# Routed expert results weighted at the copy and added up in DRAM by the scatter; absorbed weights formed in fewer, wider products

## The chip, the cores and the metric

One core of a Trainium2 chip runs the whole program in one launch. The metric is the device time of the launch in microseconds (us). The engines are named as the profile names them: PE (TensorE, matmuls; PEld its weight loads), DVE (VectorE), ACT (ScalarE), POOL (GpSimd) and SP (SyncE, which here only issues transfers); "POOLq", "SPq" and "ACTq" are what their sequencers do besides computing.

## The reference

`x` is [16, 56, 256] in float32, which is 896 tokens of 256 numbers; `ctx_512` is [16, 1500, 64]. Four layers each add a gated attention and a gated feed-forward part, both on a layer norm of `x`:

```python
x = x + tanh(g_xattn[l]) * xattn_l(layernorm(x), ctx_512, ...)
x = x + tanh(g_ffn[l])   * ffn_l(layernorm(x), ...)
```

Attention of layers 1 to 3 is over 1500 rows with 16 heads and heavily factored weights; cut to what matters:

```python
q_hk  = (hidden_q @ Wq.T).reshape(b, s, 16, 128)
q_big = einsum('bshk,hkq->bshq', q_hk, w_kc_q)      # 192 per head; layer 2 rotates it here
q_r   = einsum('bshq,hqr->bhsr', q_big, W_qr)
k_r   = einsum('bld,hdr->bhlr', kv_rope, W_kr)
attn  = softmax(einsum('bhsr,bhlr->bhsl', q_r, k_r))
ctx_c = einsum('bhsl,bld->bhsd', attn, kv_rope)
out   = einsum('bhsd,hkd->bshk', ctx_c, w_kc_kv).reshape(b, s, 2048) @ Wo.T
```

The feed-forward parts are mixtures of experts in layers 0, 2 and 3 (layer 1 has one 8-bit matrix). Layer 0 has 16 experts, the 4 best per token weighted by their softmax, plus two shared experts; layer 3 the same with weights normalised to one, and none shared:

```python
top_w, top_idx = top_k(softmax(logits), 4)
top_w = top_w / sum(top_w)                           # layer 3 only
out = sum over the 4 choices of  top_w * (silu(x @ gate_e) * (x @ up_e)) @ down_e
```

Layer 2 has 8 experts and takes the best one, weighted by a sigmoid.

## The kernel before, in words

The tokens lie in SBUF as `x`, 8 token tiles of 112 tokens. The Python program emits instructions in the order in which it is written; `in_order` and `pin` keep that order, so each engine's queue is what the loops below write, one after the other. Transfers of SP are one queue, those of POOL another.

**Absorbed weights.** `absorbing` (lines 242 to 305) makes, for a pair of heads, one matrix that takes the normalised tokens straight to the query against the rotated context. In layers 1 and 3 four products (float32, two records each in the profile) of `wqr` and `wkr` give `e` [96, 2, 2, 64] (line 280, copied by ACT at 282), four more with `wkc` give `f` (288, copied by DVE at 290), four with `wq` give `M` (297, ACT at 299); two of `wo` and `wkv` give `G` (304). In layer 2, where the rotation stands between, `Mr` is made by eight products (258, 259, ACT copies of 384 columns at 260), and `er` by four of 64 columns (265) with three ACT operations, two of which mask a half by a column of `small`. `queries` (320) calls it for group g+1 between the projections of group g (`project`, line 337); the first two or three groups are made earlier: at the end of layer 0's experts for layer 1, of layer 2's for layer 3, and in the 8-bit layer for layer 2. `load_heads` (224) loads the factors through SP.

**Routing.** `Router.token_tile` (915; layers 2 and 3) and `token_tiles` (1018; layer 0, two tiles at a time) normalise the tokens, rank the experts, count with triangular products at which place of which expert each choice stands, and copy the token's row once per choice into `xr` [112, 4, 257]: 256 numbers and one more, the number of the row (token, choice) in which the result is wanted. Four indirect transfers from POOL scatter these into `rows` in DRAM, sorted by expert (1007, 1100). Before that `clear_rows` (1151) has written zeros over `rows`, 16 transfers of 899.5 KB on SP during layer 0's attention. Behind the scatter the weight of each choice is picked (`weight`), and `finish_weights` (1143) multiplies it by the gate (in layer 3 after dividing by the sum).

**Experts.** `moe` (1159) works on tiles of 128 sorted rows. `table` says which expert a tile belongs to. Layer 0 runs 34 tiles without a condition and layer 3 runs 36; the few tiles beyond stand under a condition on the counted number, which was not met in the profiled execution (34 + 8 + 36 = 78 scatters are seen). Per tile, in a software pipeline of `tiles` (1277): SP loads `wgu`, `wd` and `xrow` three tiles ahead into four buffers each; `turn` transposes the rows (1205, ACT copy 1207) and DVE forms the destination `to` (1209: number plus a mask that pushes rows of no token out of bounds); `hidden` multiplies by gate and up (1217), ACT applies silu (1221), DVE multiplies (1222); `turn_hidden` transposes (1228, 1230); `down` multiplies (1239), ACT copies to `y` (1241, three buffers), and POOL scatters the 128 rows of 1 KB into `results` [896, 4, 256] in DRAM (1242). A bound skips rows out of range, and `declare_no_dep` states that two scatters never write the same row, so that no scatter waits for another.

**What POOL does beside it.** In layer 0 POOL also makes a part of the context's rope table (lines 874, 879, 880), one piece each third tile. In layers 0 and 3, every second one of the last tiles, it makes four diagonal matrices of a token tile's weights (1311), for the tiles in `by_pe`, 6 in layer 0 and 5 in layer 3.

**The end of the experts.** After the condition, PE makes absorbed weights of the next layer (`nxt.absorb`). SP loads `back`, eight transfers of 448 KB (1346), which wait for all scatters. `occupy` (115) issues bfloat16 products of ones that nobody reads. Then each token tile's four results are weighted and summed: tiles in `by_pe` by four products with the diagonals (1359) and a DVE addition (1369), the others by four DVE operations (1372). In layer 3 ACT's queue then sends each tile out (1374); in layers 0 and 2 `nxt.tile` (210) does the next layer norm, whose result PE transposes for the queries.

Of the kernel before, what the change touches and what calls it, by code (L numbers as in the profile page):

```python
# [47 lines left out]
H = 16  # L48
# [3 lines left out]
DQ = 192  # L52
# [6 lines left out]
DX = D + 1  # L59
FAR = 65536.0  # L60

C_U, C_BASE, C_J, C_D4, C_D1, C_ROW, C_C, C_E, C_CAND, C_P, C_M, C_H, C_N = 0, 112, 128, 132, 164, 172, 215, 216, 217, 218, 219, 221, 223
# [12 lines left out]
def flamingo_kernel(ctx: ExitStack, tc: tile.TileContext, d: dict, out: bass.AP):  # L75
# [38 lines left out]

    def occupy(n):

        ps = misc()
        for _ in range(n):
            in_order(nc.tensor.matmul(ps, onesb[:, 0:128], onesb, start=True, stop=True))
    dram = ctx.enter_context(tc.tile_pool(name="dram", bufs=1, space=bass.MemoryType.DRAM))  # L120
    rows = dram.tile([16 * CT, 128, DX], F32, name="rows")
    results = dram.tile([B * S, 4, D], F32, name="results")
# [101 lines left out]
    def load_heads(name, src, g):  # L224
# [3 lines left out]
        room = {"wkc": 512}.get(name, size)  # L228
        w = wpool.tile([128 if name == "wkc" else p, room], F32, tag=name, name=name)[0:p, 0:size]
# [12 lines left out]
    def absorbing(l, g, G, pool, made, pin):  # L242
# [6 lines left out]
        if l == 2:  # L249
# [3 lines left out]
            for k in range(2):  # L253
                ps = misc()
                for j in range(2):
                    lhsT = wq[:, j, k * 128 : (k + 1) * 128]
                    rest = ps[:, 256:384].rearrange("p (b j c) -> p j b c", b=2, j=2)[:, j]
                    pin(nc.tensor.matmul(ps[:, j * 128 : (j + 1) * 128], lhsT, wkc[:, j, 0:128], start=True, stop=True))
                    pin(nc.tensor.matmul(rest, lhsT, wkc[:, j, 128:192].rearrange("p (b c) -> p b c", b=2), start=True, stop=True))
                pin(nc.scalar.copy(M[:, k, :], ps[:, 0:384]))  # L260
                yield
            ps = misc()
            for j in range(2):
                for lhsT, o in ((wqr[:, j, :], 0), (wqr[:, 2, :], 128)):
                    pin(nc.tensor.matmul(ps[:, o + j * DC : o + (j + 1) * DC], lhsT, wkr[:, j, :], start=True, stop=True))
            e = pool.tile([128, 2, 128], F32, name="er", bufs=bufs)
            pin(nc.scalar.copy(e[:, 0, :], ps[:, 0:128]))
            for j in range(2):
                pin(nc.scalar.activation(
                    e[:, 1, j * DC : (j + 1) * DC], ps[:, 128 + j * DC : 128 + (j + 1) * DC], AF.Copy, scale=small[:, C_H + j : C_H + j + 1]  # L270
                ))
            yield
            made[g] = M, e
        else:

            ps = misc()
            for j in range(2):
                for i in range(2):
                    c = (2 * j + i) * DC
                    pin(nc.tensor.matmul(ps[0:96, c : c + DC], wqr[:, j, i * 96 : (i + 1) * 96], wkr[:, j, :], start=True, stop=True))  # L280
            e = pool.tile([96, 2, 2, DC], F32, name="e")
            pin(nc.scalar.copy(e.rearrange("p j i c -> p (j i c)"), ps[0:96, 0 : 4 * DC]))
# [3 lines left out]
            for j in range(2):  # L286
                for i in range(2):
                    pin(nc.tensor.matmul(ps[:, j * DC : (j + 1) * DC], wkc[:, j, i, :], e[:, j, i, :], start=i == 0, stop=i == 1))
# [97 lines left out]
    def attention_mha(router, roping):  # L386
        with ExitStack() as st:
# [51 lines left out]
            clear = clear_rows(ap1)  # L439
# [208 lines left out]
    def attention_mla(l, nxt, router=None, behind_queries=None):  # L648

        with ExitStack() as st:  # L650
# [173 lines left out]
            for k in range(n + 2):  # L824
# [18 lines left out]
                for i in range(6):  # L843
                    if new and i == 2:
                        new.exps1()
                        new.invert()
                    if turn:
                        turn.turned(i)
                if val and val.j == nq - 1:
# [46 lines left out]
    class Router:  # L896
# [18 lines left out]
        def token_tile(self, t):  # L915
# [12 lines left out]
            c = C_D4 + 4 * t if top == 4 else C_D1 + t  # L928
            in_order(nc.gpsimd.tensor_copy(xr[:, :, D : D + 1], small[0:TP, c : c + top].unsqueeze(2)))
# [64 lines left out]
            place = pool.tile([TP, n_e], F32, name="place")  # L994
            in_order(nc.vector.tensor_tensor(place, before, small[0:TP, C_BASE : C_BASE + n_e], ALU.add))
            yield
            is_j = pool.tile([TP, top, n_e], F32, name="is_j")
# [3 lines left out]
            in_order(nc.vector.tensor_tensor(is_j, bcast(rank, 1, top), bcast(small[0:TP, C_J : C_J + top], 2, n_e), ALU.is_equal))  # L1001
# [12 lines left out]
            in_order(nc.vector.tensor_tensor(is_j, is_j, bcast(p, 1, top), ALU.mult))  # L1014
            in_order(nc.vector.tensor_reduce(self.weight[:, t, :], is_j, AX.X, ALU.add))
            yield "end"

        def token_tiles(self, t, n):
# [20 lines left out]
            for u in range(n):  # L1039
# [3 lines left out]
                c = C_D4 + 4 * (t + u)  # L1043
                in_order(nc.gpsimd.tensor_copy(xr[:, u, :, D : D + 1], small[0:TP, c : c + top].unsqueeze(2)))
# [32 lines left out]
            self.total = so_far[n]  # L1077
            yield
# [10 lines left out]
            is_j, prod = tmp("is_j", top, n_e), tmp("prod", top, n_e)  # L1089
            place, slot = tmp("place", n_e), tmp("slot", top)  # L1090
            in_order(nc.vector.tensor_tensor(is_j, bcast(rank, 2, top), bcast(bcast(small[0:TP, C_J : C_J + top], 2, n_e), 1, n), ALU.is_equal))
# [15 lines left out]
            in_order(nc.vector.tensor_tensor(is_j, is_j, bcast(p, 2, top), ALU.mult))  # L1107
            in_order(nc.vector.tensor_reduce(self.weight[:, t : t + n, :], is_j, AX.X, ALU.add))
# [34 lines left out]
        def finish_weights(self):  # L1143
            if self.l == 3:
# [14 lines left out]
    def moe(r, nxt=None, tail=None, rest=None):  # L1159
# [5 lines left out]
        with ExitStack() as st:  # L1165
# [184 lines left out]
            def add_up(t):  # L1350

                if t not in by_pe:
                    return
# [331 lines left out]
```

## Time and profile before

| what | value |
|---|---|
| median of three runs | 2435.41 us (2428.84 to 2443.81) |
| profiled execution | 2433.22 us |
| its span | 2431.4 us, 48119 instructions |
| mean granted TensorE clock | 0.956 of full speed |
| layer 0's expert tiles, first to last scatter | 193.6 to 310.9 us (34) |
| layer 3's expert tiles, first to last scatter | 2293.6 to 2405.5 us (36) |
| diagonals on POOL (line 1311) | 44, 24.1 us |
| sums on PE (line 1359) | 88 records, 21.0 us |
| loads of `back`, layers 0 and 3 | 16 of 448 KB |

The page divides the span into 40 slices of 60.8 us and gives a digit for each engine and slice, the busy share in tenths. A group's row gives the line, engine, operation, the tiles out<-in, the count, busy us, mean ns of one, and how long the engine sat idle before and what ended it. In the chain of waits the columns are start, length and what; in rows of the trace "DMA to landing" counts from the issue of a transfer until its completion is signalled.

### The profile page before, as it was taken

The page shows a single profiled execution, that of the slowest core. Times are in us where ns is not written, and L with a number is a line of the kernel's source. Part 1 is how long each engine was busy: PE and PEld are TensorE (multiplying, and loading weights), DVE is VectorE, ACT ScalarE, POOL GpSimd, SP SyncE. Part 2 cuts the span into 40 slices and gives each one's busy share as a digit, 9 for nine tenths or more (in the row PEclk, how much of TensorE's full clock was granted, in tenths as well). Part 3 has the DMA queues.
Part 4 walks back from the last instruction along what each step waited for, and adds up shares of the span by engine and source line. Part 5 has one row for each costly group of instructions (what it writes and reads, how often), then busy time and mean ns, then how long its engine had stood idle before and what let it go on. Part 6 is the DMA issues. An engine that isn't in the chain of part 4 may idle for free. (4 is left out here: it accounts for less than half of the span.)

```text
span 2431.4 us, 48119 instructions
## 1 busy us (share of the span) xinstructions
PE 2273.1 (93%) x18034; PEld 1648.4 (68%) x18034; DVE 1507.5 (62%) x3384; ACT 1234.8 (51%) x2705; POOL 411.8 (17%) x707
## 2 busy tenths in 40 slices
PE   8678988999999998989999999979899999999687
PEld 5445665777777776447777777755577777777454
DVE  4752335667666667767777777724477777777222
ACT  4312325666666662346666666612566666665231
POOL 4454810000000001430000000001001111111223
PEclk9769988999999998999999999989899999999899
DMA  7736742000000002100000000045200000000497
GB/s 215 220 97 183 222 132 75 22 22 22 21 21 22 22 23 61 35 28 22 22 24 23 24 24 23 11 153 166 61 22 16 27 26 28 28 29 17 151 282 207
DMA packets 114115, 171.93 MB, mean 71 GB/s; under 512 B 20154, under 2 KB 75971, under 8 KB 112852
## 3 DMA queue, kind: packets, MB, share of 16 engines
q1 hardware_dynamic: 104342, 150.30, 20.4%
q0 software_dynamic: 7600, 17.14, 2.2%
q8 instruction: 145, 2.38, 0.4%
q10 hardware_dynamic: 1934, 1.34, 0.2%
q14 instruction: 94, 0.77, 0.1%
HBM read 130.19 MB, written 40.48 MB: 70 GB/s over the span
## 5 line engine op out<-in xcount | busy, mean ns | idle before, releaser
L734 ACT ACTIVATE p<-s_ps,nm 128x500 f32<-128x500 f32 x504 | 335.7, 675 | 396.8 <-DVE nm L725 396.8
L723 DVE TENSOR_REDUCE part<-s_ps 128x1 f32<-128x500 f32 x504 | 340.5, 677 | 262.9 <-PE s_ps L711 262.7
L711 PE MATMUL s_ps<-kvT,qT 64*128 64x500 f32 x2016 | 484.4, 607 | 13.7 <-ACT p L734 6.3
L785 PEld LDWEIGHTS m_ps<-pT,kv 125*64 125x64 f32 x8064 | 436.7, 137 | 76.7 <-issue 69.5
L785 PE MATMUL m_ps<-pT,kv 125*64 125x128 f32 x8064 | 477.3, 275 | 2.2 <-ACT pT L778 1.7
L711 PEld LDWEIGHTS s_ps<-kvT,qT 64*128 64x128 f32 x2016 | 185.5, 189 | 198.4 <-issue 121.1
L773 PE MATMUL m_ps<-ident,p 128*125 128x128 f32 x2016 | 299.4, 283 | 0.3
L728 DVE TENSOR_REDUCE nm<-s_ps 128x1 f32<-128x1500 f32 x168 | 287.1, 1709 | 2.3 <-PE s_ps L711 2.3
L773 PEld LDWEIGHTS m_ps<-ident,p 128*125 128x125 f32 x2016 | 249.4, 188 | 36.5 <-issue 27.0
L743 ACT ACTIVATE p<-s_ps,nm 128x1500 f32<-128x1500 f32 x168 | 254.9, 1517 | 1.3 <-DVE nm L728 0.8
L773 PE MATMUL s_ps<-ident,p 128*125 128x128 f32 x2016 | 251.3, 275 | 0.0
L754 POOL TENSOR_TENSOR den<-den 128x1 f32<-128x1 f32 x168 | 33.4, 199 | 1217.7 <-ACT p L734 1217.4
L773 PEld LDWEIGHTS s_ps<-ident,p 128*125 128x125 f32 x2016 | 237.1, 190 | 0.0
L778 ACT COPY pT<-s_ps 125x512 f32<-125x512 f32 x336 | 181.2, 598 | 90.6 <-PE s_ps L773 76.7
L778 ACT COPY pT<-m_ps 125x512 f32<-125x512 f32 x336 | 185.7, 620 | 0.0
L1217 PE MATMUL gu_ps<-wgu,xT 128*128 128x448 f32 (+2 forms) x344 | 144.0, 546 | 21.2 <-DMA wgu<-in_L_wgu 14.7
L796 DVE TENSOR_TENSOR ctxT<-m_ps,rep 64x128 f32<-64x128 f32 (+1 forms) x384 | 104.4, 272 | 88.4 <-PE m_ps L785 81.6
L1222 DVE TENSOR_TENSOR act<-gu_ps,act 128x224 f32<-128x224 f32 (+2 forms) x78 | 31.2, 400 | 193.3 <-ACT act L1221 193.3
L318 ACT COPY qT<-q_ps 64x224 f32<-64x224 f32 x128 | 71.8, 561 | 109.3 <-PE q_ps L362 71.0
L776 DVE COPY pT<-m_ps 125x512 f32<-125x512 f32 x168 | 116.2, 691 | 10.0 <-PE s_ps L773 0.4
L776 DVE COPY pT<-s_ps 125x512 f32<-125x512 f32 x168 | 114.3, 680 | 0.0
L1217 PEld LDWEIGHTS gu_ps<-wgu,xT 128*128 128x128 f32 x344 | 63.9, 195 | 72.3 <-issue 31.4
(289 smaller groups left out, 2651.2 us busy)
## 6 DMA issues: line engine op xcount, KB each, us to landing
wgu<-in_L_wgu SPq DMA_DIRECT2D x36, 448.0 KB
rows<-zero SPq DMA_DIRECT2D x16, 899.5 KB
kvT<-turned_kv SPq DMA_DIRECT2D x16, 750.0 KB
wgu<-in_L_wgu SPq DMA_DIRECT2D x34, 352.0 KB
rep<-through SPq DMA_DIRECT2D x336, 32.0 KB
xrow<-rows SPq DMA_DIRECT2D x78, 128.5 KB
wgu<-in_L_wgu SPq DMA_DIRECT2D x8, 1024.0 KB
wd<-in_L_wd SPq DMA_DIRECT2D x36, 224.0 KB
```

What stands on the lines that cost most here:

```text
L318: nc.scalar.copy(o, i)
L711: in_order(nc.tensor.matmul(o[:, 0 : 4 * KP], qT[64 * b : 64 * b + 64, t, j * QT : (j + 1) * QT], kvTs[t][64 * b : 64 * b + 64, z * 4 * KP ...
L723: in_order(nc.vector.tensor_reduce(self.part[:, z : z + 1], sp0[z][:, 0 : 4 * KP], AX.X, ALU.max))
L728: in_order(nc.vector.tensor_reduce(self.nm[1], sp1[:, :, 0 : 4 * KP], AX.XY, ALU.max, negate=True))
L734: in_order(nc.scalar.activation(self.p[0][:, 4 * z * KP : 4 * (z + 1) * KP], sp0[z][:, 0 : 4 * KP], AF.Exp, bias=self.nm[0], accum_out=sel ...
L743: in_order(nc.scalar.activation(self.p[1].rearrange("p (z c) -> p z c", z=3), sp1[:, :, 0 : 4 * KP], AF.Exp, bias=self.nm[1], accum_out=se ...
L773: in_order(nc.tensor.transpose(ps[:, c, :], self.p[b][:, k : k + KP], ident))
L776: in_order(nc.vector.tensor_copy(o, ps))
L778: in_order(nc.scalar.copy(o, ps))
L785: in_order(nc.tensor.matmul(self.pv[64 * b : 64 * b + 64, :], kv[:, self.t, c, b, :], self.pT[:, c, b, :], start=c == 0, stop=c == KC - 1))
L796: in_order(nc.vector.tensor_tensor(ctxs[self.t][64 * a : 64 * a + 64, b, lo - 448 * a : hi - 448 * a], self.pv[64 * b : 64 * b + 64, cols] ...
L1217: in_order(nc.tensor.matmul(ps[:, s, 0:n], xT[:, k, :], wgu[:, k, s * n : (s + 1) * n], start=k == 0, stop=k == 1))
```

## The change

In layers 0 and 3 (`SUMMED`) the row that is scattered to the experts carries two numbers beside its values: the token's number and the choice's weight. ACT's copy of `y` multiplies by that weight, taken from the row's last column. The scatter then adds into DRAM, into one of two sums of [1024, 256] that start as zeros, tile i into sum i % 2. Rows of no token go to 128 spare rows behind the 896. The declaration of no dependence is gone for these scatters, since different choices of a token meet in one row: each scatter waits for the landing of the earlier one into the same sum, that is of the tile two before; the program's order of instructions shows this wait in POOL's queue.

At the end of the experts two transfers of 224 KB per pair of token tiles bring the sums back (eight in all), POOL adds the two sums of a pair, and DVE multiplies by the gate (layer 3: gate over the sum of weights) and adds to `x`, one operation per token tile. The diagonals, PE's sums, and layer 3's 30 products of `occupy` are gone. Layer 2 keeps the plain scatter, into [896, 1, 256], and takes the same loop in pairs.

The router picks the weights before it uses the places: in layer 3 two DVE operations and a POOL copy more ahead of the scatter of rows, in layer 0 ahead of the counting products. Four clears of 1.05 MB are added on SP: two before the clears of `rows`, two inside layer 1's attention. `xrow` has seven buffers instead of four.

The absorbed weights: in layers 1 and 3 `wqr` and `wkc` are multiplied first, four products of 128 columns, two heads side by side, and one product with a block-diagonal `wkr` replaces the other four. In layer 2 four products of 192 columns and two of 128 replace eight and four, with five ACT copies per group as before (four of them smaller, one of 256 columns), and no masking.

The diff, cut to its core:

```diff
-DX = D + 1
+DX = D + 2
+SUMMED = (0, 3)
...
-    results = dram.tile([B * S, 4, D], F32, name="results")
+    results = dram.tile([B * S, 1, D], F32, name="results")
+    summed = {l: [dram.tile([B * S + 128, D], F32, name=f"summed{l}{i}") for i in range(2)] for l in SUMMED}
...
             for k in range(2):
-                ps = misc()
+                ps = misc()[:, 0 : 2 * DQ].rearrange("p (j c) -> p j c", j=2)
                 for j in range(2):
-                    lhsT = wq[:, j, k * 128 : (k + 1) * 128]
-                    rest = ps[:, 256:384].rearrange("p (b j c) -> p j b c", b=2, j=2)[:, j]
-                    pin(nc.tensor.matmul(ps[:, j * 128 : (j + 1) * 128], lhsT, wkc[:, j, 0:128], start=True, stop=True))
-                    pin(nc.tensor.matmul(rest, lhsT, wkc[:, j, 128:192].rearrange("p (b c) -> p b c", b=2), start=True, stop=True))
-                pin(nc.scalar.copy(M[:, k, :], ps[:, 0:384]))
+                    pin(nc.tensor.matmul(ps[:, j, :], wq[:, j, k * 128 : (k + 1) * 128], wkc[:, j, :], start=True, stop=True))
+                pin(nc.scalar.copy(M[:, k, 0:256].rearrange("p (j c) -> p j c", j=2), ps[:, :, 0:128]))
+                rest = M[:, k, 256:384].rearrange("p (b j c) -> p j b c", b=2, j=2)
+                pin(nc.scalar.copy(rest, ps[:, :, 128:DQ].rearrange("p j (b c) -> p j b c", b=2)))
...
-            for j in range(2):
-                for i in range(2):
-                    c = (2 * j + i) * DC
-                    pin(nc.tensor.matmul(ps[0:96, c : c + DC], wqr[:, j, i * 96 : (i + 1) * 96], wkr[:, j, :], start=True, stop=True))
-            e = pool.tile([96, 2, 2, DC], F32, name="e")
+            for i in range(2):
+                for j in range(2):
+                    pin(nc.tensor.matmul(
+                        ps[64 * j : 64 * j + 64, 0:128], wqr[:, j, i, :], wkc[:, j, i, :], start=i == 0, stop=i == 1, skip_group_check=True
+                    ))
+            e = pool.tile([128, 128], F32, name="e")
...
-            for j in range(2):
-                for i in range(2):
-                    pin(nc.tensor.matmul(ps[:, j * DC : (j + 1) * DC], wkc[:, j, i, :], e[:, j, i, :], start=i == 0, stop=i == 1))
+            pin(nc.tensor.matmul(ps[:, 0 : 2 * DC], e, wkr[:, 0, :], start=True, stop=True))
...
+                if l == 1 and k == 8:
+                    for o in summed.get(3, []):
+                        clear_sum(o)
...
+            in_order(nc.vector.tensor_tensor(is_j, bcast(rank, 1, top), bcast(small[0:TP, C_J : C_J + top], 2, n_e), ALU.is_equal))
+            if l in SUMMED:
+                in_order(nc.vector.tensor_tensor(is_p, is_j, bcast(p, 1, top), ALU.mult))
+                in_order(nc.vector.tensor_reduce(self.weight[:, t, :], is_p, AX.X, ALU.add))
+                in_order(nc.gpsimd.tensor_copy(xr[:, :, D + 1 : D + 2], self.weight[:, t, :].unsqueeze(2)))
...
+    def clear_sum(o):
+        in_order(nc.sync.dma_start(o.rearrange("(n p) c -> p n c", p=128), bcast(zero[:, 0:D], 1, 8)))
...
-                in_order(nc.vector.tensor_scalar(to, xt[:, D : D + 1], r.mask[:, i : i + 1], None, ALU.add))
-                return xT, to
+                spare = (small[:, C_SPARE : C_SPARE + 1], ALU.add, ALU.min) if l in SUMMED else (None, ALU.add)
+                in_order(nc.vector.tensor_scalar(to, xt[:, D : D + 1], r.mask[:, i : i + 1], *spare))
+                return xT, to, xt[:, D + 1 : D + 2]
...
+                if l in SUMMED:
+                    in_order(nc.scalar.activation(y, ps, AF.Copy, scale=weight))
+                    in_order(nc.gpsimd.indirect_dma_start(summed[l][i % 2], place, y, None, compute_op=ALU.add))
+                    return
                 in_order(nc.scalar.copy(y, ps))
...
-                    diag[t] = pd.tile([TP, top, TP], F32, name=f"diag{t}")
-                    for j in range(top):
-                        in_order(nc.gpsimd.tensor_scalar(diag[t][:, j, :], ident[0:TP, 0:TP], r.weight[:, t, j : j + 1], None, ALU.mult))
...
-            for t in range(NT):
-                back.append(pt.tile([TP, top, D], F32, name="back"))
-                in_order(nc.sync.dma_start(back[t], flat[t * TP * top : (t + 1) * TP * top].rearrange("(p j) c -> p j c", j=top)))
-            occupy({0: 4, 2: 20, 3: 30}[l])
+            for t in range(0, NT, 2):
+                back[t] = pt.tile([TP, 2, 2, D], F32, name="back")
+                for i, o in enumerate(summed[l] if l in SUMMED else [flat]):
+                    in_order(nc.sync.dma_start(back[t][:, i], o[t * TP : (t + 2) * TP].rearrange("(u p) c -> p u c", u=2)))
+            occupy({0: 4, 2: 20, 3: 0}[l])
+            for t in range(0, NT, 2):
+                y = back[t][:, 0]
+                if l in SUMMED:
+                    in_order(nc.gpsimd.tensor_tensor(y, y, back[t][:, 1], ALU.add))
+                for u in range(2):
+                    in_order(nc.vector.scalar_tensor_tensor(x[:, t + u, :], y[:, u], r.factor[t + u], x[:, t + u, :], ALU.mult, ALU.add))
```

## The prediction

> **What bounds the kernel now.** I read the page's busy rows first, then the rows of 40 slices, the chain of waits, windows of the stages that the change touches, and the instructions in those windows in order of time. All sums are made against the profiled execution: 2433.2 us, of which 2431.4 are the span and 1.8 lie around it. The median of the three runs is 2435.4, so I add 2.2 at the end.
>
> ```profile
> PE 2273.1 (93%) x18034; PEld 1648.4 (68%) x18034; DVE 1507.5 (62%) x3384; ACT 1234.8 (51%) x2705; POOL 411.8 (17%) x707
> POOL 4454810000000001430000000001001111111223
> DMA  7736742000000002100000000045200000000497
> ```
>
> PE is busy 93% of the span, but the last two slices (60 us each) have DMA at 9 and 7 while PE falls to 6 and 8. POOL's only 8 is the slice of layer 0's expert tiles. So each stage needs its own look. Columns of the windows: window, length, then busy us of PE, PEld, DVE, ACT, POOL, then the granted clock, the DMA share and GB/s.
>
> ```profile
> 283.00:293.00 10.00, 9.85 (x46) 7.56 (x47) 3.43 (x11) 3.15 (x9) 9.38 (x12) 1.00 0.76 229
> 365.00:375.00 10.00, 10.00 (x58) 6.32 (x57) 3.52 (x7) 4.82 (x11) 0.00 (x0) 1.00 0.47 144
> 2345.00:2355.00 10.00, 9.36 (x41) 6.04 (x40) 2.79 (x10) 3.72 (x11) 2.92 (x3) 1.00 0.92 291
> ```
>
> In order: layer 0's tiles have POOL (9.38) and PE (9.85) both full; layer 1's queries, where absorbed weights are made between projections, are PE alone (10.00 of 10); layer 3's tiles have PE at 9.36 with DMA at 0.92. The end of layer 3 is a chain of transfers:
>
> ```profile
> 2402.91 0.98 POOL results L1242
> 2404.20 4.57 DMA results<-y,to
> 2410.70 9.41 DMA back<-results
> 2420.24 5.42 PE sum_ps L1359 x24
> 2427.57 0.48 DVE x L1372
> ```
>
> A scatter lands after 4.57, eight loads of 448 KB take some ten us, the last sums follow. From the last scatter's issue (2405.5) to the end of the span are 25.9 us.
>
> **The change, part by part.**
>
> *Scatter that adds.* The scatter's price is its landing, counted from the issue. In the window of layer 3's tiles, and in that of layer 0's (min/median/max):
>
> ```profile
> L1242 POOL DMA_INDIRECT results<-y,to x36: 968/974/1034, 2293.6 to 2405.5; - x36
> DMA to landing us min/median/max: 2.1/4.3/5.6
> ```
>
> ```profile
> DMA to landing us min/median/max: 2.1/3.7/5.2
> ```
>
> Now each scatter waits in POOL's queue for the landing of the one two before it (same sum). So two tiles take at least L + 0.3 (0.3 is the gap seen between neighbouring scatters), one tile (L+0.3)/2. Tiles come every 3.55 us in layer 0 (34 from 193.6 to 310.9) and every 3.20 in layer 3. The new wait is free in layer 3 below L = 6.1. In layer 0 the limit by this is 6.8, but POOL also carries a 3.6 us piece of the rope table at every third tile (11 pieces), behind which one of the two chains stands; I count 0.7 us a piece (an estimate, a fifth of its length) once L passes 5. What queues behind a waiting scatter is the next scatter and the rope pieces. The y buffers (three) come free at a landing, so ACT's copy waits next, then PE for its PSUM; only then does the wait reach the end.
>
> L itself: no accumulating transfer is in the trace. From below it is 3.7 to 4.3, the same scatter without addition, if the destination's read hides in the write. Here a rule must be weighed. The Trainium skill ("DMA: Bandwidth & Descriptors", Anatomy of one DMA) prices a transfer from GpSimd at 2.0 us plus bytes/436e3, for 128 KB 2.3 us; "HBM Reference", Latency, has an access at 0.2 us on average and 2 under high load. By them an adding scatter lands at 2.5 to 4.3, and the chain never binds. The trace has 2.3 only as its minimum (2.1, when the queues are empty); the loaded medians are 3.7 and 4.3, so I take the row and put the page's access on it: 3.9 (idle) to 6.3 (high load). I take 5.0, nearer the 4.57 of the chain's row. By the row with 6.3, layer 3 would lose 36 x 0.1 = 3.6; by the page's own numbers, nothing.
>
> *Bytes.* All 128 rows are now written instead of some 100 (3584 of 36 x 128), and each is read too. Layer 3's tile moves 448 + 224 + 128.5 + 100 = 900 KB before, some 1057 after, at a mean share of 0.91: 0.91 x 1057/900 = 1.07, over 1. PE already waited for wgu there (8.0 us in all). If the read costs no engine time, the share is 0.94 and the loop stays; in full, the period rises by 7% of 3.2, 8 us over 36 tiles, and 10 with the wait in place. Range 0 to +10, taken +5. Layer 0's share is 0.44 to 0.78: +2 for chain and traffic (0 to +4).
>
> *Layer 0's tail.* Diags go (24 of 0.55 us on POOL, 13 us), and PE's sums. Before, the sums stood behind absorb products at half clock:
>
> ```profile
> 318.00:319.00 1.00, 1.00 (x7) 1.00 (x6) 0.00 (x0) 0.25 (x1) 0.00 (x0) 0.50 0.95 270
> 326.00:327.00 1.00, 1.00 (x6) 0.84 (x5) 0.16 (x1) 0.00 (x0) 0.00 (x0) 1.00 1.00 262
> ```
>
> DVE's first add ran at 326.84, its last statistics at 342.5, and projections were full from 346. After, the loads carry 1.83 MB, not 3.67: the first pair (448 KB) can be there some 2 us after its issue at 314.95, POOL adds 112x512 in 1.3 (between the rows 0.8 for 112x256 and 1.8 for 125x768), so DVE starts near 319 to 321. A pair costs DVE 2 x (0.49 product + 0.43 + 0.18 statistics) + 0.3 + 0.73 = 3.25, four pairs 13: done at 332 to 334, normalised, turned and copied by 336.5 rather than 346: -9.5. What it may lose is the clock: the Trainium skill ("TensorE: Matmul & The Clock Gate", Part 1) opens the gate after one busy window of some 3.4 us. By the rule the sixteen busy us from 309 should have opened it; the row shows 0.50 for all of them, and 1.00 only after the four 512-wide products at 322. By the rule the transposes, now without sums between them, cost nothing; by the row a half-clocked start of the queries costs up to 3.4/2 = 1.7. Before has the like (PE idle 342 to 345, then 0.50 from 347 to 349), so I count no difference. Bounds -5 and -12.
>
> *Absorbed weights.* In the queries, eight records of L280 take 0.89 us and eight of L288 1.00, all in PE's path. After: eight records twice as wide but of the same count (0.86, by L280's own 0.11) and two of 128 wide (0.22): 0.8 less a group. Six groups in layer 1's queries -4.8, five in layer 3's -4.0. Layer 2's twelve products per group become six, but its copies on ACT (0.48 twice, then 0.37 and 0.27 twice) stand in the same path: -0.25 for eight groups, -2. Layer 2's tail has two groups at half clock ahead of the transposes: -1.5. Together -12.3; bounds -6 and -16, as ACT or DVE may show up behind PE.
>
> *Small terms.* Two clears of 1.05 MB ahead of the first rows: 2.1 MB at 265 GB/s is 8 us, but POOL sat idle there 9.65 and 14.4 us for other reasons: +1 (0 to 8). Layer 3's two clears lie inside attention with DMA at 0 to 2 tenths: 0; without that cover 8. Layer 3's router gets two DVE operations (0.22) and a POOL copy (0.19) ahead of the last scatter of rows: +0.5. Turning y's copy into a scaled one: 0. Ranking work in layer 0 only changes place: 0.
>
> *Layer 3's tail.* Before 25.9 from the last scatter. After: landing 5.0, SP 0.3, 1.83 MB at 280 GB/s 6.5 plus a first-byte time of 2, POOL's last add 1.3, two products 1.0, and the same 3.35 from DVE's last to the end: 19.4. That is -6.5; PE's 20 sums and 30 filler products are gone, but they only filled the wait. Bounds -4 and -8.
>
> Sum: +2 - 9.5 - 12.3 + 1 + 0.5 + 5 - 6.5 = -19.8. Profiled 2413.4, on the scale of the median 2415.6: 2415.
>
> **Rivals.**
>
> A, *the chain of scatters becomes the bound.* For it: POOL at 9.38 of 10 in layer 0, landings already up to 5.6, and transfers that are near their limit in layer 3, which lengthen L itself. Against: two sums, and a median that leaves 1.8 us in layer 3. At L = 7: layer 0 34 x 0.1 + 11 x 0.7 = 11, layer 3 36 x 0.45 = 16; instead of the +7 counted this is +27, sum 0: 2435. At L = 8: 28 and 34, 2471. It decides from L = 7 on (no gain), and from 7.7 costs over 1%.
>
> B, *nothing is paid in the loops.* The read hides in the landing, the share stays below 1; POOL, relieved of 24.1 us of diags, is early. For it: PE is at 9.36 in layer 3's tiles with all landings behind it. Sum -26.8: 2408.5.
>
> C, *the transfers bind.* Layer 3's loop +10, layer 0's +4, the front +4, L near 6: sum -8: 2428. For it: 0.92 of share and wgu waits; against: wgu is issued three tiles ahead and xrow now has seven buffers.
>
> D, *the tails don't shrink.* Layer 0's tail gives 5 and layer 3's 4, if the two halves of a pair arrive late and POOL's adds line up: 2422.
>
> **How the numbers follow.** Likeliest (with D as its upper end) 0.50: 2415, own range 2406 to 2424; B 0.25; C 0.14; A 0.11, half of it over 1% slower. About 1% (24 us) is what a measurement of this kernel can tell from no change, so faster means below 2411. Of the likeliest case a third lies there (0.17), of B some 85% (0.21), and of the rest nothing: 0.38. Slower (over 2460) is half of A: 0.06, 0.07 with the front's 8 us. The rest is 0.55. The range leaves out a tenth below 2401 (B with gains at their bounds) and a tenth above 2436 (A past L = 7).
>
> **What would show it.** The landing of the adding scatter in both stages, near 5; in layer 3's tiles a POOL wait for an earlier scatter that is short, and a period of 3.2 to 3.4; DMA share at 0.95 to 1.0; layer 1's groups at 5.7 us instead of 6.5; DVE's first product of layer 0's tail before 322; 19 to 20 us from the last scatter to the end. Wrong it would be if scatters follow each other at (L+0.3)/2 with L over 6.5, if PE's wait for wgu grows past 20 us, or if the queries don't shorten because copies follow each other there.

## The result, and the profile after

The changed kernel takes 2411.94 us (median of 6 runs, 2408.96 to 2418.02) against 2431.95 before (6 runs): the ratio is 0.9915, with a 95% interval from 0.9888 to 0.9942. Ratios are formed from fast runs alone; there was one slow run, of 3756.70 us, among the nine of `e7_three_sums` below, whose median counts it. The forecast was 2415 (2401 to 2436), most likely within 1%. The profiled execution has a span of 2408.4 us, 23.0 less than before. So the number held. How it comes about did not: the routed part, for which I had counted 7.5 us of gain, gives nothing, and the absorbed weights give more than I counted.

First the page of the changed kernel: busy time, and POOL and DMA in 40 slices.

```profile
PE 2220.4 (92%) x17724; PEld 1598.3 (66%) x17724; DVE 1500.8 (62%) x3367; ACT 1239.5 (51%) x2705; POOL 441.0 (18%) x687
...
POOL 6355720000000001430000000001001111111344
...
DMA  7637842100000002100000000044200000000597
```

PE has 310 records and 53 us less to do, but POOL has 29 us more, with all 44 diagonals (24 us) gone. The next rows answer to the three windows shown of before (layer 0's tiles, layer 1's queries, layer 3's tiles), with the same columns:

```profile
283.00:293.00 10.00, 10.00 (x44) 7.39 (x43) 3.49 (x11) 3.02 (x8) 7.87 (x6) 0.87 0.86 199
359.00:369.00 10.00, 10.00 (x52) 5.44 (x52) 4.18 (x9) 5.40 (x13) 0.00 (x0) 1.00 0.48 150
2323.00:2333.00 10.00, 8.26 (x35) 5.23 (x34) 2.65 (x9) 3.35 (x9) 4.56 (x4) 1.00 1.01 282
```

In layer 3's tiles the DMA share goes from 0.92 to 1.01 while GB/s fall from 291 to 282 and PE's busy time from 9.36 to 8.26: the transfers are full, and PE waits. In layer 0 the share is 0.86 instead of 0.76, at 199 GB/s instead of 229. Then the chain that ends the program:

```profile
2382.73 4.65 DMA summed<-y,to
...
2388.14 3.61 DMA summed<-y,to
...
2393.64 5.72 DMA back<-summed
...
2399.43 1.27 POOL back L1368
...
2400.73 1.89 DVE x L1370 x2
```

The loads take 5.72 us where they took 9.41, but now a scatter stands in the chain behind a scatter: the last one was issued at 2388.14, when the one of 2382.73 had landed.

The span by stretches, each from one event to the next in both profiles (layer 0's first scatter of a result at 193.6 and 192.7, and so on):

| stretch | before | after | difference | counted |
|---|---|---|---|---|
| start to layer 0's first scatter | 193.6 | 192.7 | -0.9 | +1 |
| layer 0's tiles, first to last scatter | 117.3 | 122.4 | +5.1 | +2 |
| to layer 1's first whole group of absorbed weights | 35.1 | 30.5 | -4.6 | -9.5 |
| to its first score product | 48.6 | 43.2 | -5.4 | -4.8 |
| layer 1's attention | 520.2 | 520.0 | -0.2 | 0 |
| 8-bit layer, to layer 2's first projection | 40.9 | 33.2 | -7.7 | part of -2 |
| to layer 2's last scatter of rows | 649.4 | 648.9 | -0.5 | rest of -2 |
| layer 2's experts, to the last scatter | 65.3 | 61.2 | -4.1 | 0 |
| to layer 3's first projection | 18.5 | 19.2 | +0.7 | -1.5 |
| layer 3's queries | 45.3 | 42.5 | -2.8 | -4 |
| layer 3's attention and router | 540.7 | 538.8 | -1.9 | +0.5 |
| to the first scatter of a result | 18.8 | 18.8 | 0 | 0 |
| layer 3's tiles, first to last scatter | 111.9 | 116.7 | +4.9 | +5 |
| to the end of the span | 25.9 | 20.3 | -5.6 | -6.5 |

Two rows are mostly not the change's doing. The first part of layer 2's experts, from the last scatter of rows to the first of results, took 32.5 us before and 27.6 after; of the kernels below with the same products there, two took 27.1 and 27.4 and eight 31.6 to 31.8. From layer 3's last projection to its last score product the kernels range from 499.5 to 503.3 us, whatever was changed (before 503.3, after 500.1). So I count some 7 us as chance of the profiled pair, which is 3 us further apart than the medians (23.0 against 20.0). The rest of layer 3's row goes the other way: from the last score product to the last scatter of rows the router takes 38.7 us in each of the six kernels with the adding scatter, and 37.4 in before (37.4 or 37.5 in four of the five others with the plain scatter, 39.0 in e1).

### The profile page after: what moved, and what is told of

It is laid out like the page before. It is cut to its first block, busy times and chain, and to the rows that moved or that the text cites. A ratio compares the mean times of both kernels' runs of the same rounds, so it can differ in the third digit from the quotient of the medians.

```text
span 2408.4 us, 47484 instructions
## 1 busy us (share of the span) xinstructions
PE 2220.4 (92%) x17724; PEld 1598.3 (66%) x17724; DVE 1500.8 (62%) x3367; ACT 1239.5 (51%) x2705; POOL 441.0 (18%) x687
## 5 line engine op out<-in xcount | busy, mean ns | idle before, releaser
L1241 PE MATMUL gu_ps<-wgu,xT 128*128 128x448 f32 (+2 forms) x344 | 141.8, 539 | 26.2 <-DMA wgu<-in_L_wgu 19.2
L1268 POOL DMA_INDIRECT summed<-y,to x70 | 109.9, 1570 | 131.1 <-ACT y L1267 80.4
```

The lines of the kernel that those rows point to most:

```text
L1241: in_order(nc.tensor.matmul(ps[:, s, 0:n], xT[:, k, :], wgu[:, k, s * n : (s + 1) * n], start=k == 0, stop=k == 1))
L1268: in_order(nc.gpsimd.indirect_dma_start(summed[l][i % 2], place, y, None, compute_op=ALU.add))
```

## The experiments

All ratios are to the kernel before, run beside each, with 95% intervals.

**The two halves of the change alone.** `e1_absorb_only` is before with only the new products:

```diff
-pin(nc.tensor.matmul(ps[0:96, c : c + DC], wqr[:, j, i * 96 : (i + 1) * 96], wkr[:, j, :], start=True, stop=True))
+pin(nc.tensor.matmul(
+    ps[64 * j : 64 * j + 64, 0:128], wqr[:, j, i, :], wkc[:, j, i, :], start=i == 0, stop=i == 1, skip_group_check=True
+))
...
-pin(nc.tensor.matmul(ps[:, j * DC : (j + 1) * DC], wkc[:, j, i, :], e[:, j, i, :], start=i == 0, stop=i == 1))
+pin(nc.tensor.matmul(ps[:, 0 : 2 * DC], e, wkr[:, 0, :], start=True, stop=True))
```

> The kernel before with the absorbed weights of the change alone (fewer, wider products in layers 1 to 3); routing, scatter, sums as before. Theory A, that nearly all of the change's 20 us comes from these products, their help to the clock in the 8-bit layer included: 16 to 20 us less than before. Theory B, that the gain is shared as predicted (12 from the products, 8 from the routed part): 10 to 13 us less. In the trace A expects the stretch after the pause at the start of the 8-bit layer at full clock again within 4 us, B the half clock of before.

Measured: 2409.09 (2431.28 before), 0.992 (0.9901 to 0.994): by the ratio 19.5 us less. `e2_routed_only` is the opposite, the changed kernel with the old products:

> The changed kernel with the absorbed weights of before: the adding scatter, the two sums and the short tails alone. Theory A: 0 to 5 us less than before, since what the tails give (5 each) the tiles take back (5 each). Theory B: 7 to 10 us less.

Measured: 2434.69, 1.0025 (1.0005 to 1.0046): by the ratio 6 us more than before, worse than either theory had it. Theory A holds, and further than I had put it: all of the gain is from the absorbed weights, and the routed part on the old products loses. The halves do not add up to the whole: -19.5 and +6 against the change's -20, and the changed kernel's ratio, 0.9915, is no worse than e1's. Whether the routed part loses beside the new products too is shown by e11 and e12 below.

**What the scatter loses.** `e3_no_chain` scatters as before does, but with the weighted copy and the short loads:

```diff
-in_order(nc.gpsimd.indirect_dma_start(summed[l][i % 2], place, y, None, compute_op=ALU.add))
+i = nc.gpsimd.indirect_dma_start(apart[l], place, y, None, bounds_check=B * S * 4 - 1, oob_is_err=False)
+for o in sent:
+    tc.declare_no_dep(i.ins, o.ins, reason="different rows: a token's choice has one place")
```

> The changed kernel with the scatter of before (each choice to a row of its own, no addition, rows of no token skipped, no wait for an earlier scatter), weighted copy and loads of 1.83 MB as in the change. It leaves the adding up of the four choices out: it reads back two of four rows per token, of other tokens. Theory A, that the chain of adding scatters costs what it seems to in both stages of tiles: 8 to 11 us less than the changed kernel, periods of 3.5 and 3.2 us per tile, layer 0's last scatter before 312. Theory B, that the chain lies in cover and the tiles are slower for another reason (the transfers' bytes): at most 4 us less than the changed kernel.

Its total (2430.26, 0.9993, 0.9977 to 1.0009) can't be compared: the left-out sums change what later layers route, and layer 2 ran 14 tiles instead of 8. Its stretches can. Layer 0's tiles take 110.0 us (122.4 in the changed kernel), layer 3's 111.1 (116.7). `e4_chain_plain` keeps the chain and the rows of no token, and only overwrites:

```diff
-in_order(nc.gpsimd.indirect_dma_start(summed[l][i % 2], place, y, None, compute_op=ALU.add))
+in_order(nc.gpsimd.indirect_dma_start(summed[l][i % 2], place, y, None))
```

> The changed kernel with the scatter into the two sums by turns, each waiting for the one two before and all 128 rows written, but overwriting instead of adding: the destination is not read, and the last choice stays instead of the sum. If the time is that of reading and adding (a longer landing): 5 to 9 us less than the changed kernel, landings of 4 us. If it is the wait for any landing at all, or the rows of no token: within 3 us of the changed kernel.

Measured: 2398.29, 0.9875 (0.9852 to 0.9897), with the tile counts of before: about 10 us less than the change by the ratios (13.7 by the medians). Layer 0's tiles take 117.5, layer 3's 114.0, and DVE's wait for landings in layer 0 falls from 41.6 to 7.1 us. So the adding costs some 10 us of the total. In the profiled stretches it is 4.9 and 2.7 us of the way from e3 to the changed kernel, and the chain with the written rows of no token 7.5 and 2.9; this split is rough, since e4's profiled execution (2406.01) is the slowest of its four. How the adding shows in the transfers is in the row of GpSimd's queue (packets, MB, share of 16 engines' span), in the changed kernel and then in e4:

```profile
q0 software_dynamic: 14320, 19.00, 4.1%
```

```profile
q0 software_dynamic: 7600, 19.00, 2.4%
```

The same megabytes are written, but 6720 packets more pass, 96 for each of the 70 scatters, and 1.7% of 2408 us is 41 us of all 16 engines, 0.58 us a scatter (an estimate, from rounded shares). With layer 3's share at 0.85 in e4 and tiles every 3.2 us, that would be 0.18 more, which fills the engines. The windows over layer 3's tiles, the changed kernel's and e4's, have 0.97 and 0.85:

```profile
2271.00:2388.00 117.00, 98.92 (x403) 61.64 (x401) 32.34 (x99) 40.43 (x101) 54.68 (x35) 1.00 0.97 260
```

```profile
2271.00:2385.00 114.00, 99.79 (x404) 61.41 (x402) 30.09 (x99) 40.49 (x101) 33.90 (x35) 1.00 0.85 265
```

**Is it the wait, or what is behind it?** In the changed kernel's layer 3 POOL seems to wait for DVE. `e5_more_buffers`:

```diff
-to = pp.tile([128, 1], I32, name="to", bufs=5)
+to = pp.tile([128, 1], I32, name="to", bufs=8)
-y = pp.tile([128, D], F32, name="y")
+y = pp.tile([128, D], F32, name="y", bufs=5)
```

> The changed kernel with eight buffers for the destinations and five for y, instead of five and three. In the changed kernel DVE waited 41.6 us (layer 0) and 21.9 us (layer 3) for landings before it could write a destination, and ACT 10.4 us before it could write y, and behind them stand the next tile's products. If these borrowed waits are how a landing reaches the end: 4 to 8 us less than the changed kernel, with layer 3's period back from 3.34 to 3.2 us. If the chain itself (POOL's wait) sets the pace: within 2 us, and the wait only moves to POOL.

Measured: 2418.08, 0.9943 (0.9923 to 0.9963), no gain; layer 3's tiles 120.5. The second theory was right, and the two rows of waits (us, times, longest), the changed kernel's and then e5's, show why:

```profile
POOL summed L1268 <- DVE to L1233: 36.7, 17, 3.0
```

```profile
POOL summed L1268 <- DMA summed<-y,to: 32.6, 14, 3.4
```

With five buffers the destination of tile i+1 reuses that of tile i-4, which is the very scatter that scatter i-2 waits for; DVE only ended last. With eight the row names what was waited for. `e7_three_sums` loosens the chain:

```diff
-summed = {l: [dram.tile([B * S + 128, D], F32, name=f"summed{l}{i}") for i in range(2)] for l in SUMMED}
+summed = {l: [dram.tile([B * S + 128, D], F32, name=f"summed{l}{i}") for i in range(3)] for l in SUMMED}
...
+for i in (1, 2):
+    in_order(nc.gpsimd.tensor_tensor(y, y, back[t][:, i], ALU.add))
```

> The changed kernel with three sums by turns (each scatter waits for the one three before; 12 loads come back and POOL adds twice per pair). If the chain of waits is what the adding scatter costs: layer 0's last scatter at 311 instead of 315, layer 3's tiles 4 us shorter, 2 to 3 us of both given back in each tail: 2 to 5 us less than the changed kernel. If it is the reading of the destination as such: 3 to 6 us more.

Measured: 2419.77, 0.9946 (0.9926 to 0.9966), no better. The layers part company. Layer 0's tiles take 113.9 instead of 122.4: there it was the chain. Layer 3's take 118.4 instead of 116.7, with the DMA engines as full as in the changed kernel, 0.97 (the window over its tiles):

```profile
2271.00:2388.00 117.00, 99.78 (x402) 61.00 (x400) 32.41 (x99) 40.26 (x100) 53.55 (x35) 1.00 0.97 257
```

There it is the transfers; the landings, too, got longer with one more scatter allowed on its way (median 6.5 us in layer 3, against 5.7 to 6.0 in the kernels with two sums whose traces hold them). What layer 0 gained went into the tails: from its last scatter to layer 1's first score product 80.2 us instead of 73.7, from layer 3's last scatter to the end 25.7 instead of 20.3.

`e8_rope_on_dve` takes the other work out of POOL's queue:

```diff
-yield from self.parts(t)
+yield from self.parts(t, nc.vector)
```

> The changed kernel with layer 0's pieces of the rope table (11 of 3.5 to 4.2 us between scatters) on DVE instead of POOL. If the pieces, standing in POOL's queue between two links of the chain, make layer 0's tiles late: last scatter at 311 instead of 315 and 3 to 5 us less than the changed kernel. If not: the same, or up to 5 us more where DVE keeps PE waiting.

Measured: 2409.16, 0.9913 (0.9891 to 0.9935). Layer 0's last scatter comes at 307.8 (315.1), layer 1's first score product at 382.0 (388.8), but the total can't be told from the change's 0.9915. Inconclusive.

**The clock in the 8-bit layer.** `e6_before_filler` leaves the products of before as they are and fills the pause:

```diff
+def fill():
+    ps = ps_o.tile([TP, D], F32, name="o_ps")
+    for _ in range(36):
+        in_order(nc.tensor.matmul(ps, onesb[:, 0:TP], onesb[:, 0:D], start=True, stop=True))
```

> The kernel before with 36 filler products (bfloat16, 256 columns, never read) put into PE's queue where it pauses 4.6 us at the start of the 8-bit layer, behind the first two of eight products of absorbed weights. If the extra gain there (7.6 us of the 13.6 by which the changed kernel is early at layer 2's first projection) is the clock, which stays at half for 16 us after that pause: 4 to 7 us less than before, with full clock from 921 us on. If it is the count of products: no less than before, 0 to 4 us more.

Measured: 2424.12, 0.9977 (0.9966 to 0.9988), 5.6 us less than before, with 36 products more. Windows of before, of the changed kernel, and of this one:

```profile
921.00:926.00 5.00, 4.82 (x22) 4.71 (x22) 4.72 (x12) 1.46 (x4) 0.00 (x0) 0.50 0.00 0
926.00:932.00 6.00, 5.38 (x25) 3.60 (x24) 2.75 (x6) 2.65 (x9) 0.00 (x0) 0.50 0.49 136
932.00:939.00 7.00, 6.38 (x22) 4.69 (x23) 3.56 (x12) 0.53 (x1) 0.00 (x0) 0.65 0.44 148
```

```profile
915.00:921.00 6.00, 5.75 (x24) 4.99 (x24) 5.65 (x14) 2.60 (x11) 0.00 (x0) 0.55 0.10 31
921.00:926.00 5.00, 3.71 (x22) 2.64 (x19) 3.71 (x10) 1.68 (x4) 0.00 (x0) 1.00 0.86 267
```

```profile
921.00:926.00 5.00, 5.00 (x48) 5.00 (x48) 4.64 (x19) 0.61 (x3) 0.00 (x0) 1.00 0.00 0
926.00:932.00 6.00, 5.18 (x44) 4.35 (x42) 5.62 (x16) 3.37 (x12) 0.00 (x0) 1.00 0.06 8
```

Before, PE paused 4.6 us for an ACT copy and then ran products of 64 to 256 columns at half clock, though busy about 90%. Read in finer windows the clock is 0.50 from 919.9 to 936.8, 16.9 us, and as long in e2, which has the old products too; in the changed kernel and in e1 it is 0.50 for some 7 us. The filler keeps it open throughout, and with it the stretch to layer 2's first projection takes 32.7 us with the old products, against 40.9 in before and 33.2 in the changed kernel. So the extra gain there is the clock; that it is the width and not the smaller number of records that opened it sooner is only argued.

**Can the halves be parted for a better kernel?** Four more, on one chip beside the same runs of before: the absorbed weights alone with the rope pieces on DVE (e9), with 14 fillers ahead of the condition in layer 0 (e10), with both (e11); and the changed kernel with both (e12).

```diff
+            if l == 0:
+                occupy(14)
             live = nc.values_load(...)
```

> The kernel before with the new absorbed weights, and layer 0's rope pieces on DVE instead of POOL; routed part as before. If POOL sets layer 0's pace without the chain too (it was busy 9.38 of 10 us): last scatter at 303 to 305 instead of 307 to 311, 3 to 6 us less than with the absorbed weights alone, a ratio near 0.990 to before. If the pieces matter only under the chain of adding scatters: no less than with the absorbed weights alone.

> The kernel before with the new absorbed weights, and 14 filler products (bfloat16, 512 columns, never read) on PE ahead of the condition at the end of layer 0's tiles, where PE sat idle 3.6 us and then ran its narrow products at half clock for 8 us and more. If the idle stretch closes the clock: full clock through the absorbed weights there, these in 4.2 us instead of 8.2, and 3 to 5 us less than with the absorbed weights alone. If the back loads set layer 0's tail anyway: the products are earlier and the end within 1 us.

> The absorbed weights of the change, rope pieces on DVE and the filler, routed part as before: the sum of the two, 5 to 9 us less than the absorbed weights alone, which is 0.988 to 0.990 of before. If both give the same cover back only once: 3 us.

> The changed kernel with rope pieces on DVE and the filler. If the routed part of the change pays once layer 0's POOL is free: 1 to 3 us less than the same two edits with the routed part as before, since layer 0's tail is shorter and only layer 3's tiles still lose. If layer 3's loss (tiles about 9 us longer by the add's traffic, tail 5.6 shorter) decides: 2 to 5 us more.

| kernel | median, us | ratio to before (2428.45) |
|---|---|---|
| e9: absorbed weights, rope on DVE | 2399.67 | 0.9881 (0.9858 to 0.9903) |
| e10: absorbed weights, filler | 2402.68 | 0.9892 (0.9868 to 0.9917) |
| e11: absorbed weights, both | 2400.05 | 0.9882 (0.9859 to 0.9904) |
| e12: the changed kernel, both | 2408.03 | 0.9922 (0.9897 to 0.9946) |

e11 and e12 differ in the routed part alone: with the adding scatter the kernel is 8.0 us slower (the six runs of each don't overlap: 2395.07 to 2401.05, 2404.23 to 2415.38). The profiled pair, 12.9 us apart, shows where. Layer 3's tiles take 121.7 instead of 114.0 us and its tail 20.4 instead of 24.4; layer 0's tiles take 118.8 instead of 112.8. Layer 2, whose scatter doesn't add, loses as well: from its last scatter to layer 3's first projection are 17.2 us instead of 14.3 (14.3 or 14.4 in e1, e9 and e10, 16.8 to 19.4 in the other adding kernels with the new products). DVE's first addition there, in e11 and in e12, comes 4.8 and 7.7 us behind the last scatter (of 1647.59 and 1650.97):

```profile
1652.42 0.48 DVE L1369 SCALAR_TENSOR_TENSOR x<-back,weight,x 112x256 f32<-112x256 f32 x1 [2.04 <-DMA back<-results]
```

```profile
1658.64 0.48 DVE L1373 SCALAR_TENSOR_TENSOR x<-back,red,x 112x256 f32<-112x256 f32 x1 [4.06 <-DMA back<-results]
```

The last scatter landed after 2.4 us in e11 and 4.7 in e12, and the first load is now of two token tiles. The loads in pairs alone are not it, since e3 has them too and takes 14.3 us; why the landing is longer is open. And the windows over layer 0's tail, first e11, then e12, show a cost that nobody had counted:

```profile
305.00:335.00 30.00, 24.70 (x123) 16.55 (x122) 15.89 (x50) 6.97 (x16) 0.86 (x1) 0.94 0.77 191
```

```profile
308.00:340.00 32.00, 14.60 (x59) 8.07 (x58) 16.84 (x46) 7.33 (x17) 6.59 (x5) 0.70 0.51 122
```

With the sums on PE (24.7 us of work in all) the clock there is 0.94; without them PE has 14.6 us, and the clock is 0.70, with half clock where the queries begin. The other kernels with the new products agree: over 30 to 32 us there, 0.83 to 1.00 with the sums (e1, e9, e10), 0.63 and 0.72 without (the changed kernel, e8). But busy time alone doesn't keep the clock open: in before, sums included, PE is busy 24.9 of the 30 us from 305 at a clock of 0.72, with the old narrow products. In time it takes back what the shorter tail gives: from layer 0's last scatter to layer 1's first score product are 76.5 us in e11 and 77.0 in e12. By their ratios e9 and e11 are 8 us below the changed kernel (the intervals just overlap), and 8 us below e12, which stands for it here: these are the best versions that compute everything. Why e9 and e10 are faster than e1 is left open: e9's last scatter of layer 0 comes no earlier than e1's (307.4 and 307.3), against what I expected, and e1's profiled execution was its fastest (2396.76), so it doesn't show where its others lose. The two edits do not add up. The filler of e10 did keep the clock open (1.00 from 304 to 315.5; the absorbed weights there in 5.0 us instead of e1's 8.1), but then the sums waited 4.1 us for `back`, so in its profile the loads set the tail.

## Why the prediction was right or wrong

*The total* was right by luck in its parts: routed part -7.5 counted, +6 measured alone (e2); absorbed weights -12.3 counted, -19.5 measured alone (e1). Two errors in opposite directions met near the number.

*The landing, "I take 5.0"*, is the first term that failed. In layer 3 (start, us, engine, line; first POOL, then DVE):

```profile
2315.98 1.56 POOL L1268 DMA_INDIRECT summed<-y,to  x1 [1.92 <-DVE to L1233]
2318.58 1.56 POOL L1268 DMA_INDIRECT summed<-y,to  x1 [1.04 <-ACT y L1267]
2322.07 1.56 POOL L1268 DMA_INDIRECT summed<-y,to  x1 [1.93 <-DVE to L1233]
```

```profile
2321.34 0.27 DVE L1233 TENSOR_SCALAR to<-xrow,mask,small 128x1 int32<-128x1 f32 x1 [0.94 <-DMA summed<-y,to]
```

DVE's wait ends when the scatter of 2315.98 has landed, 5.36 us after its issue, and right after it POOL goes on with the next scatter to that sum. Read so at all 21 such waits of layer 3, the landing is 5.1 to 7.2 us, 6.1 in the middle; the other 15 landed before anyone waited, so this is the slower part of them. The traces of e5 and e8, which have two sums too, hold most landings of layer 3 themselves (32 and 27 of 36). The median is 5.7 us in e8, and in e5:

```profile
DMA to landing us min/median/max: 3.7/5.9/7.3
```

So it lies nearer the upper bound (6.3) than 5.0, and close to the break-even that I had named for layer 3 (6.1). The Trainium skill's "HBM Reference", Latency, gave that bound with its 2 us under high load; the row plus that figure (4.3 + 2) was the better guide, though no run shows that the added time is that access, and my choice of 5.0 by the chain's 4.57 was wrong: that row was taken at the end of the stage, where the DMA share was down to 0.11 (2404 to 2409). There the adding scatters land in 4.65 and 3.61, too. The fit in "DMA: Bandwidth & Descriptors", Anatomy of one DMA (2.3 us), is less than half of these medians.

*Layer 3's tiles, "+5"*: +4.9 in the profiled pair, right in size and cause (bytes: e7 shows that loosening the chain doesn't help, e4 that not adding gives more than half of it back). PE's wait for wgu grew from 8.0 to 12.2 us, short of the 20 that I had named. Over all profiles the loss is more: 116.7 to 121.8 us in the six kernels that add, 109.5 to 114.0 in the six that scatter plainly (before, e1, e6, e9, e10, e11). The issue itself grew, which I had not counted: 1.56 us on POOL instead of 0.97.

*Layer 0's tiles, "+2"*: +5.1, and it was the chain (e7: 113.9) under POOL's rope pieces (e8: 115.8), at landings of 3.7 to 6.6 us (medians 5.1 and 5.4 in e5 and e8).

*Layer 0's tail, "done at 332 to 334 ... by 336.5"* is the step that failed most. SP's first load, POOL's first sum and DVE's first product, after the last scatter:

```profile
315.07 1.57 POOL L1268 DMA_INDIRECT summed<-y,to  x1 [1.09 <-ACT e L283]
324.43 1.26 POOL L1368 TENSOR_TENSOR back<-back 112x512 f32<-112x512 f32 x1 [7.79 <-DMA back<-summed]
```

```profile
320.53 3.89 SPq L1363 DMA_DIRECT2D back<-summed  x8
```

```profile
325.72 0.48 DVE L1370 SCALAR_TENSOR_TENSOR x<-back,gates,x 112x256 f32<-112x256 f32 x1 [10.07 <-POOL back L1368]
```

I had kept the loads' issue at 314.95, where it was before. But the last scatter is 4.2 late and takes 1.4 longer to its landing, so they start at 320.53; the first pair is with POOL 3.9 us behind that, where I had counted 2; and DVE starts at 325.72, 1.1 earlier than before instead of 6 to 8. From there to the first whole group of absorbed weights are 19.8 us (before 19.1), not the 16 that I counted: DVE's four pairs took 13 as counted (to 339), but its last statistics stand in its queue behind copies of queries, and these wait for projections at half clock:

```profile
336.00:341.00 5.00, 4.38 (x10) 2.00 (x9) 3.57 (x12) 0.67 (x2) 0.00 (x0) 0.58 0.01 4
```

The transposes before them, with pauses between, did not open the clock. The projections themselves, of 448 columns, did so after 3.3 us (0.51 from 336.9 to 340.2, 1.00 behind), as the rule of one busy window in "TensorE: Matmul & The Clock Gate", Part 1, has it. For the narrow products the rule is too kind: in before PE was busy for all of 310.6 to 325.8 at 0.50, and nearly all of 921 to 932 in the 8-bit layer. "I count no difference" held against before, but not against what the tail could have been: e11 with e12.

The tail was also credited to the wrong half. The two groups of absorbed weights ahead of it, whose shorter products I had counted for layer 2's tail but not here, took 6.5 us before for their first two steps and 2.9 after, mostly at half clock. In e1, where scatter and sums are those of before, DVE's first addition comes 12.4 us behind the last scatter, and in e11 10.5, against 16.0 in before and 10.7 in the changed kernel.

*Absorbed weights*: in the queries 1.89 us a group became 1.12 (0.66 and 0.46), 0.77 less where I had 0.8; layer 1's queries -5.4 (-4.8), layer 3's -2.8 (-4). What was missed, beside layer 0's tail, is the 8-bit layer, -7.7 where layer 2 had -2 in all; I had costed products at full clock and not looked at the clock of the stretch they stand in. Layer 2's tail shows the -1.5 only without the routed part, and more of it: 14.3 or 14.4 us in e1 and e9 to e11, against 18.5 in before and 19.2 in the changed kernel.

*Layer 3's tail, "-6.5"*: -5.6. *Clears*: nothing seen (-0.9 to layer 0's first scatter). *Layer 3's router, "+0.5"*: 1.3 us.

*Rivals*: C (transfers bind, L near 6) describes the routed part best, B failed outright, A is what layer 0 does, at a landing below the 7 from which I had it decide, since POOL's rope pieces and 1.56 us issues leave less room than the formula.

## What to carry to other kernels

A DMA that adds moves work from the end of a stage into its loop, and pays there in landing time, in DMA engine time and in POOL's issue; here, with the loop's transfers already at a share of 0.85, the shorter tail did not pay for it. Test the halves of a change apart: here one half carried all of the gain and the other hid a loss of 6 to 8 us in the total. Before products are costed, look at the clock granted in their window, and before "idle filler" or matmuls in a tail are removed, at who keeps the clock open.

## What the runs showed of the hardware that was not expected

- An indirect scatter of 128 rows of 1 KB with addition took POOL 1.56 us to issue, without 0.97; 96 packets more per scatter and, by estimate, 0.58 us more of all 16 DMA engines, at the same megabytes written.
- Its landing in layer 3's tiles had medians of 5.7 and 5.9 us (3.7 to 7.3; e8, e5), and still took 3.6 and 4.65 us at the end of the stage; the plain one had a median of 4.3 (2.1 to 5.6).
- PE, about 90% busy with products of 64 to 256 columns, stayed at a granted clock of 0.50 for 11 us (921 to 932), and at a mean of 0.65 over the next 7, after a pause of 4.6 us; 36 filler products of 256 columns in the pause kept it at 1.00.
